# Two self-attention blocks of a perceiver kernel put into one hand-written schedule, batch by batch

## The chip, the cores and the metric

The kernel runs on one core of a Trainium2 chip. Its time is the device time in microseconds (us) of one execution; where several executions were timed, their median. One more execution was recorded by the hardware profiler: the profile has a record of every instruction on each engine. TensorE (PE in the profile) does the matrix products and transpositions, VectorE (DVE) and ScalarE (ACT) elementwise work and reductions, GpSimd (POOL) elementwise work on SBUF alone, SyncE (SP) asks for the transfers. Each engine works through its own list of instructions in the order of the program, and waits on semaphores for what others produce.

## What is computed

Six blocks in a row change an activation `x` of 4 batches x 256 tokens x 256 features, all in float32. The first four (a cross attention, a small self attention across batches, a mixture of experts, a second cross attention over 4096 keys) are not touched. The last two, cut to what matters:

```python
# fifth block, on z = _layernorm(x)
x_norm = layer_norm(z, g1, beta1)
q, k, v = heads(x_norm @ Wq + bq), heads(x_norm @ Wk + bk), heads(x_norm @ Wv + bv)   # 16 heads of 16
q, k = apply_rope(q), apply_rope(k)
attn = jax.nn.softmax(jnp.einsum('bhqd,bhkd->bhqk', q / jnp.sqrt(hd), k), axis=-1)
y = z + jnp.einsum('bhqk,bhkd->bhqd', attn, v) @ Wo + bo
x = x + y + jax.nn.relu(layer_norm(y, g2, beta2) @ W1 + b1) @ W2 + b2
# sixth block, on z = _layernorm(x): the same attention without the rotation, then a mixture of 8 experts
y = z + layernorm(attention(z) @ Wo + bo, g1, be1)
gate_probs = jax.nn.softmax(y @ Wg + bg, axis=-1)
top_vals, top_idx = jax.lax.top_k(gate_probs, 2)
x = x + y + layernorm(sum over the two of top_vals * (y @ We[e] + bexp[e]), g2, be2)
```

## The kernel before

Tokens lie in 8 tiles of 128, two to a batch. The blocks run one after the other (`build`, L1280), and the fifth and sixth are `l1_attn` (L1115) and `l1_ffn` (L1190). Each works stage by stage over all 8 tiles: norm, transposition, projections, attention, output projection, norm, and then the feed-forward network or the experts. Outside the attention the order of the instructions is left to a scheduler; inside `manual_schedule` it is the order in which the program writes them.

A norm (`normed`, L183) takes statistics of each tile on DVE (L190, L191), an inverse root for all tiles at once (`rsqrt`, L167: an addition, a Sqrt on ACT at L174, a reciprocal and one step of correction, L175 to L180), and applies both (L194). The Sqrt needs other activation tables than the exponential, so the program has ACT_TABLE_LOAD instructions on ACT. `transposed` (L202) turns tiles on TensorE.

`self_attention` (L306) goes through 16 units, one for each batch and each group of four heads. A step of its loop has two halves (`quad`, L316): in each, TensorE computes the scores of two heads of unit i (L327) and, for two heads of unit i + 2, the products from which DVE takes negated maxima (L333, L340). The exponentials follow on ACT (L338). Between the halves TensorE turns the maxima of unit i + 1 and the shares of an older unit (`turned`, L287), DVE adds the maxima to the queries (qm, L373), and the sums of unit i - 2 are formed (`sums`, L290, with a copy on POOL at L301). After the second half the probabilities of unit i - 1 weigh the values (`weigh`, L345). In PSUM three banks rotate for the scores, three (`mm_tile`) for everything that is called mm, which the maxima share with all projections, and one each for `acc` and `nm`. The output projection (`project_out`, L386) of two tiles at a time is the only other work inside the loop.

In `l1_attn` the rotation (`rotated`, L1128) multiplies with two weights each, adds biases and turns on DVE (L1146), and adds on POOL (L1156, L1157). The matrix products of all projections are recorded at one line, L165 in `contract`. In `l1_ffn` the affine part of a norm runs on POOL and DVE (L1217 to L1219), the gates are a softmax and a choice of two (`top2`, L222), and the experts' results are added on DVE (L1267). The output is written in one transfer at the end (L1289).

## Time and profile before

| | us |
|---|---|
| median of 3 runs | 2502.66 |
| lowest and highest | 2499.27, 2503.89 |
| the profiled execution: its time | 2499.59 |
| the profiled execution: its span | 2497.8 |
| last matrix product of the block before the two | 1996.8 |
| attention of the fifth block | about 2065 to 2158 |
| attention of the sixth block | about 2271 to 2357 |

A float32 product is recorded as two instructions, so counts of matrix products are twice those of the program. In a row of the timeline stand the start, the duration, the engine, line and operation, what is written and read, and in brackets how long the engine had been idle before it and who ended that. In the table by windows each engine's busy time stands with its number of instructions, then the share of its full clock that TensorE was granted (PEclk), the mean busy share of the transfer engines, and GB/s.

### The profile page before, as it was taken

Reading aid. Unit: us, or ns where it says so; the run is one execution under the profiler, and the core shown is the slowest. Engines: PE = TensorE matmul, PEld = TensorE weight load, DVE = VectorE, ACT = ScalarE, POOL = GpSimd, SP = SyncE. Lnnn points to the kernel's source line nnn. Section 1 sums busy time; section 2 is a strip of 40 time slices with the busy share of each in tenths; the row PEclk is TensorE's granted clock in tenths of the full one; section 3 lists DMA queues with packets and bytes.
Section 4 is the critical chain, followed back from the end, with each engine's and each line's share of the span. In section 5 each row is a group of like instructions: output and inputs, shape, how many; then the busy total and the mean of one; then the engine's idle time right before and its main releaser. Section 6 shows DMA issues by size and latency. Waiting matters only on the chain.

```text
span 2497.8 us, 45306 instructions
## 1 busy us (share of the span) xinstructions
PE 2276.8 (91%) x19032; PEld 1357.6 (54%) x19032; DVE 1204.5 (48%) x2197; ACT 948.1 (38%) x1838; POOL 147.6 (6%) x263
## 2 busy tenths in 40 slices
PE   7999983799997699999999999999999979899976
PEld 5777751487774245445544555455544536565642
DVE  2221248601222286666666666666666156525555
ACT  1100010122332326665566656665555604314400
POOL 0000000120001000000000000000000032100022
PEclk9888985599998899999999999999999987999968
DMA  4112011710112411221022101211100020010000
GB/s 133 56 51 68 17 64 49 272 66 15 34 32 63 131 53 40 66 62 36 27 62 62 45 27 45 70 54 36 32 23 2 2 76 10 1 43 1 2 1 17
DMA packets 82272, 121.36 MB, mean 49 GB/s; under 512 B 5371, under 2 KB 52243, under 8 KB 82068
## 3 DMA queue, kind: packets, MB, share of 16 engines
q1 hardware_dynamic: 80532, 114.25, 14.7%
q0 software_dynamic: 1536, 4.20, 0.5%
q8 instruction: 151, 2.47, 0.4%
q14 instruction: 53, 0.43, 0.1%
HBM read 109.19 MB, written 9.24 MB: 47 GB/s over the span
## 4 chain that ended last, share of the span: by engine, by line
PE 85%; DVE 6%; issue 3%; POOL 2%; ACT 2%; DMA 1%; SPq 0%; DVEq 0%; POOLq 0%; ACTq 0%
PE sc L1001 13%; PE acc L1052 10%; PE mx L1014 8%; PE h L165 8%; PE v L909 5%; PE k L909 5%; PE gram L425 5%; PE ro L165 4%; PE we L165 2%; PE eo L165 2%; PE po L165 2%; PE kv L165 2%; PE sc L327 2%; PE xo L165 1%; PE q L165 1%
## 5 line engine op out<-in xcount | busy, mean ns | idle before, releaser
L1043 DVE TENSOR_REDUCE mx<-mx 128x1 f32<-128x512 f32 x988 | 636.5, 686 | 408.8 <-PE mx L1014 368.2
L1039 ACT ACTIVATE probs<-sc 128x512 f32<-128x512 f32 x988 | 536.8, 597 | 420.5 <-PE mx L1014 394.3
L1001 PE MATMUL sc<-qm,kT 32*128 32x256 f32 x3952 | 579.1, 400 | 8.8 <-ACT probs L1039 8.8
L1014 PE MATMUL mx<-kT,x_q 32*128 32x512 f32 x1976 | 559.2, 639 | 0.0
L1001 PEld LDWEIGHTS sc<-qm,kT 32*128 32x128 f32 x3952 | 351.3, 184 | 254.9 <-ACT probs L1039 129.0
L1052 PE MATMUL acc<-probs,v 128*32 128x256 f32 x4096 | 274.9, 385 | 0.0
L1052 PEld LDWEIGHTS acc<-probs,v 128*32 128x32 f32 x4096 | 107.2, 109 | 134.3 <-issue 89.4
L1014 PEld LDWEIGHTS mx<-kT,x_q 32*128 32x128 f32 x1976 | 149.8, 183 | 8.1 <-issue 7.6
L909 PE MATMUL k<-slab,x_wk 128*32 128x512 f32 x1024 | 137.7, 623 | 12.3 <-DMA slab<-in_ctxT 7.4
L909 PE MATMUL v<-x_wv,slab 128*32 128x256 f32 x2048 | 137.0, 385 | 0.0
L425 PE MATMUL gram<-ctx 128*128 128x257 f32 x512 | 113.8, 381 | 3.6 <-POOL kv L454 2.4
L210 PE MATMUL tr<-ident,xn 128*128 128x128 f32 x112 | 30.0, 432 | 93.7 <-DVE xn L585 40.7
L425 PEld LDWEIGHTS gram<-ctx 128*128 128x128 f32 x512 | 96.1, 190 | 18.9 <-issue 2.9
L340 DVE TENSOR_REDUCE negm<-mx 128x2 f32<-128x512 f32 x128 | 82.9, 686 | 38.8 <-PE mx L333 38.1
L255 ACT ACTIVATE kT<-k,cols 128x512 f32<-128x512 f32 x128 | 92.8, 783 | 22.5 <-PE k L909 22.5
L301 POOL COPY wide<-rec 128x256 f32<-128x256 f32 x48 | 19.1, 399 | 1354.2 <-DVE rec L299 1354.2
L338 ACT ACTIVATE probs<-sc 128x512 f32<-128x512 f32 x128 | 69.7, 595 | 67.5 <-PE mx L333 56.5
L909 PEld LDWEIGHTS v<-x_wv,slab 128*32 128x32 f32 x2048 | 53.4, 109 | 73.0 <-issue 44.2
L165 PE MATMUL h<-f_w_all,rT 128*128 x184 | 83.0, 594 | 0.7 <-DVE rT L799 0.6
L165 PE MATMUL ro<-f_w_all,hT 128*128 x368 | 83.3, 379 | 0.1
L823 ACT ACTIVATE hT<-hT,place 128x128 f32<-128x128 f32 x184 | 49.9, 383 | 77.8 <-PE hT L820 77.7
L210 PEld LDWEIGHTS tr<-ident,xn 128*128 128x128 f32 x112 | 20.7, 211 | 102.6 <-issue 46.4
(325 smaller groups left out, 2718.2 us busy)
## 6 DMA issues: line engine op xcount, KB each, us to landing
slab<-in_ctxT SPq DMA_DIRECT2D x96, 512.0 KB
ctx<-in_ctx SPq DMA_DIRECT2D x16, 1024.0 KB
f_w_all<-in_f_W_r SPq DMA_DIRECT2D x16, 1024.0 KB
w<-in_f_W_s SPq DMA_DIRECT2D x4, 1024.0 KB
f_rows<-f_zero SPq DMA_DIRECT2D x1, 2944.0 KB
row<-f_rows SPq DMA_DIRECT2D x23, 128.0 KB
f_results<-y SPq DMA_DIRECT2D x23, 128.0 KB
kT<-x_away SPq DMA_DIRECT2D x128, 8.0 KB
```

The source lines that it names most:

```text
L165: nc.tensor.matmul(out, w, m, start=i == 0, stop=i == len(pairs) - 1)
L210: nc.tensor.transpose(ps[:, k * P : (k + 1) * P], src[:, 4 * q + k, c * P : (c + 1) * P], self.ident)
L255: nc.scalar.activation(dst, ps, AF.Identity, bias=b, scale=own)
L338: nc.scalar.activation(probs[i, j], sc[j][:, 0, :], AF.Exp, scale=0.25)
L340: nc.vector.tensor_reduce(negm[i2 % 2][:, :, 32 * j + UNIT_MAX[i2 % 2]], bd[j].rearrange("p (t s) -> p t s", s=S), AX.X, ALU.max, negate=True,
L425: nc.tensor.matmul(prod[:, m, : D + 1], t[:, c, m * P : (m + 1) * P], t[:, c, :], start=n == 0 and c == 0, stop=n == 3 and c == 7,)
L909: nc.tensor.matmul(out[own], w[:, own], m, start=start, stop=not start, tile_position=(0, 32 * j))
L1001: nc.tensor.matmul(into[:, c * S : (c + 1) * S], kT[b, u, at // HALF][rows, at % HALF : at % HALF + P], qm[un][rows, :], start=True, stop= ...
L1014: nc.tensor.matmul(into, q[rows, b, u, t * P : (t + 1) * P], kT[b, u, at // HALF][rows, at % HALF : at % HALF + SLAB], start=True, stop=True,)
L1039: nc.scalar.activation(probs[j], sc[j], AF.Exp, scale=0.25)
L1043: nc.vector.tensor_reduce(mx[un2][:, k2 % 2, j, k2 // 2 : k2 // 2 + 1], bd[j], AX.X, ALU.max)
L1052: nc.tensor.matmul(acc[32 * j : 32 * j + 32, :S], v[b, chunk // VC][:, at : at + 32], probs[j][:, c * S : (c + 1) * S], start=k == 0 and c ...
```

## The change

`self_attention`, `l1_attn` and `l1_ffn` go, with `project_heads` and `values_of_tokens`, and `l1_self` takes their place. It is one `manual_schedule` for both blocks. All weights of both are asked for at its start. The attention loop is the same as before in its matrix products, but it has 32 units in a row: the 16 of the fifth block, then the 16 of the sixth. All other work of a batch is written as three generators: `before_first` (norms, transposition, rotated queries and keys, values), `after_first` (output projection, norm, feed-forward, norm of the sixth block, its projections) and `after_second` (output projection, norm, gates, experts, last norm, output of two tiles). Each `yield` ends a piece, and gives its planned TensorE time and the planned delay until the next piece of the same generator may follow.

A small planner chooses while the program is written. `now` is a clock of planned times: a half step counts 1.07, the turning and sums 1.0, weighing 1.0. Between the two halves of a step, `between(7.0)` takes pieces that are due, from the first three generators, until 7 us are planned or none is due. `through` takes pieces until a given generator is done, before the first step that needs it. Steps are counted from -2 to 35 (two before the first unit, four after the last).

Norms are taken for the two tiles of a batch. Their inverse root is exp(-0.5 ln(v)) on ACT with the same step of correction on DVE (`inverse_root`). The second norm of the fifth block's input takes its variance from the first one's instead of statistics of its own. Transpositions are evacuated by ACT alone. Of the experts' results the odd ones are scaled by ACT and added by POOL; the affine part of the last norms works on both tiles at once. The output leaves in four transfers.

```diff
-    def self_attention(self, pool, q, k, v, out, project):
...
-    def values_of_tokens(self, pool, w, xT):
...
-    def l1_attn(self, x):
...
-    def l1_ffn(self, x):
...
+    def l1_self(self, x, out):
...
+            names = ("a1_wq", "a1_wqs", "a1_wk", "a1_wks", "a1_wv")
+            wq1, wqs1, wk1, wks1, wv1 = (self.load_w(pool, n) for n in names)
             turns = self.load(pool, "turns", [P, 2, 2, S], a["turns"].rearrange("p (h t s) -> p h t s", h=2, t=2))
...
+            def inverse_root(var, eps=EPS):
+                shape = [P, var.shape[1]]
+                new = lambda i: pool.tile(shape, F32, tag=f"ir{i}", name=self.name(f"ir{i}"), bufs=3)
+                ve, s, r, t = (new(i) for i in range(4))
+                nc.vector.tensor_scalar(ve, var, eps, None, ALU.add)
+                nc.scalar.activation(s, ve, AF.Ln)
+                nc.scalar.activation(r, s, AF.Exp, scale=-0.5)
+                nc.vector.tensor_mul(t, r, r)
+                nc.vector.tensor_mul(t, t, ve)
+                nc.vector.tensor_scalar(t, t, -0.5, 1.5, ALU.mult, ALU.add)
+                nc.vector.tensor_mul(r, r, t)
+                return r
+            def moments(src):
+                stats = pool.tile([P, NB, 6], F32, tag="st", name=self.name("st"), bufs=3)
+                mv = pool.tile([P, NB, 2], F32, tag="mo", name=self.name("mo"), bufs=3)
+                for t in range(NB):
+                    nc.vector.bn_stats(stats[:, t, :], src[:, t, :])
+                    nc.vector.bn_aggr(mv[:, t, :], stats[:, t, :])
+                return mv, inverse_root(mv[:, :, 1])
+            def apply(src, mv, r, dst):
+                for t in range(NB):
+                    nc.vector.tensor_scalar(
+                        dst[:, t, :], src[:, t, :], mv[:, t, 0:1], r[:, t : t + 1], ALU.subtract, ALU.mult
+                    )
...
+            def rotated(dst, ws, biases, xT, m, one):
+                ps = self.mm_tile("ro")
+                for i, w in enumerate(ws):
+                    heads(w, xT, m, ps[:, i * S : (i + 1) * S])
+                for half in range(2):
+                    u = 2 * m + half
+                    ts = []
+                    for i, bias in enumerate(biases):
+                        t = tile(f"ro{i}", [P, S], 2)
+                        nc.vector.scalar_tensor_tensor(
+                            t, ps[:, i * S : (i + 1) * S], self.col(bias, u), turns[:, half, i], op0=ALU.add, op1=ALU.mult
+                        )
+                        ts.append(t)
+                    if one:
+                        nc.gpsimd.tensor_scalar(ts[1], ts[1], self.col("one", half), None, ALU.add)
+                    nc.gpsimd.tensor_add(dst[:, u, :], *ts)
...
+            def before_first(b):
+                z = zs[0, b] = tile("z", [P, NB, D], 5)
+                mv, r = moments(own(b))
+                apply(own(b), mv, r, z)
+                vz = pool.tile([P, NB], F32, tag="vz", name=self.name("vz"), bufs=3)
+                nc.vector.tensor_mul(vz, r, r)
+                nc.vector.tensor_mul(vz, vz, mv[:, :, 1])
+                r2 = inverse_root(vz)
+                zn = tile("n", [P, NB, D], 4)
+                for t in range(NB):
+                    nc.scalar.activation(zn[:, t, :], z[:, t, :], AF.Copy, scale=r2[:, t : t + 1])
+                yield 0.0, 9.0
+                zT = turn(zn, "a1_g1", "a1_be1")
+                yield 0.5, 1.5
+                q[0, b], k[0, b] = (tile(n, [P, UNITS, S], 3) for n in "qk")
+                for m in range(DC):
+                    rotated(q[0, b], (wq1, wqs1), ("a1_bq", "a1_bqs"), zT, m, False)
+                    yield 1.8, 0.0
+                    rotated(k[0, b], (wk1, wks1), ("a1_bk", "a1_bks"), zT, m, True)
+                    yield 1.8, 0.0
+                values((0, b), wv1, zT)
+                yield 1.8, 4.0
+            def after_first(b):
+                ps = projected((0, b), wo1, ob1)
+                y = tile("y", [P, NB, D], 2)
+                nc.vector.tensor_add(flat(y), ps, flat(zs.pop((0, b))))
+                nc.gpsimd.tensor_add(flat(own(b)), flat(y), flat(own(b)))
+                mv, r = moments(y)
+                yn = tile("n", [P, NB, D], 4)
+                apply(y, mv, r, yn)
+                yield 4.4, 7.0
...
+                nc.vector.tensor_add(flat(own(b)), ps, flat(own(b)))
+                z = zs[1, b] = tile("z", [P, NB, D], 5)
+                mv, r = moments(own(b))
+                apply(own(b), mv, r, z)
+                yield 3.9, 6.0
...
+            def after_second(b):
+                ps = projected((1, b), wo2, ob2)
+                o = tile("n", [P, NB, D], 4)
+                nc.scalar.copy(flat(o), ps)
+                both = lambda n: affine[:, n, :].unsqueeze(1).to_broadcast([P, NB, D])
+                def affine_norm(src, n, residual, dst):
+                    mv, r = moments(src)
+                    nc.gpsimd.tensor_tensor(residual, residual, both(n + 1), ALU.add)
+                    apply(src, mv, r, src)
+                    nc.vector.tensor_tensor(src, src, both(n), ALU.mult)
+                    nc.gpsimd.tensor_tensor(dst, src, residual, ALU.add)
+                y = tile("y", [P, NB, D], 2)
+                affine_norm(o, 0, zs.pop((1, b)), y)
+                yield 4.4, 9.0
+                yT = turn(y)
+                nc.gpsimd.tensor_tensor(own(b), own(b), y, ALU.add)
...
+                nc.vector.tensor_add(flat(moe), flat(moe), flat(other))
+                affine_norm(moe, 2, own(b), own(b))
+                nc.sync.dma_start(out[:, NB * b : NB * (b + 1), :], own(b))
+                yield 0.0, 0.0
...
+            now, tasks = [0.0], []
+            def begin(work, key):
+                tasks.append([work, now[0], key])
+            def piece(task):
+                try:
+                    cost, lag = next(task[0])
+                    now[0] += cost
+                    task[1] = now[0] + lag
+                except StopIteration:
+                    tasks.remove(task)
+                    return False
+                return True
+            def between(time):
+                end = now[0] + time
+                while now[0] < end:
+                    ready = [t for t in tasks[:3] if t[1] <= now[0]]
+                    if not ready:
+                        break
+                    piece(ready[0])
+            def through(key):
+                while any(t[2] == key for t in tasks):
+                    at = next(i for i, t in enumerate(tasks) if t[2] == key)
+                    ready = [t for t in tasks[: at + 1] if t[1] <= now[0]]
+                    if ready:
+                        piece(ready[0])
+                    else:
+                        now[0] = min(t[1] for t in tasks[: at + 1])
+            UN = 2 * B * UNITS
+            where = lambda i: ((i // (B * UNITS), i // UNITS % B), i % UNITS)
...
+            with self.tc.manual_schedule():
+                for b in range(B):
+                    begin(before_first(b), ("first", b))
+                through(("first", 0))
+                for i in range(-2, UN + 4):
+                    if i + 2 < UN:
+                        (side, b), u = where(i + 2)
+                        if u == 0:
+                            through(("first", b) if side == 0 else ("mid", b))
+                    quad(i, True)
+                    ps = self.ps_o.tile([P, 512], F32, tag="f", name=self.name("nm"))
+                    if 0 <= i + 1 < UN:
+                        maxima = self.turned(ps, negm[(i + 1) % 2])
+                    if 0 <= i - 3 < UN:
+                        shares = self.turned(ps[:, S:], recs.pop(i - 3))
+                    if 0 <= i + 1 < UN:
+                        key, u = where(i + 1)
+                        qm[i + 1] = tile("qm", [P, S], 2)
+                        nc.vector.tensor_add(qm[i + 1], maxima, q[key][:, u, :])
+                    if 0 <= i - 3 < UN:
+                        key, u = where(i - 3)
+                        if u == 0:
+                            att[key] = tile("att", [P, UNITS, S], 2)
+                        nc.vector.tensor_mul(att[key][:, u, :], os.pop(i - 3), shares)
+                    if 0 <= i - 2 < UN:
+                        recs[i - 2] = self.sums(pool, accs.pop(i - 2), os[i - 2])
+                    now[0] += 1.0
+                    if 0 <= i - 3 < UN:
+                        (side, b), u = where(i - 3)
+                        if u == UNITS - 1:
+                            begin(after_first(b) if side == 0 else after_second(b), ("mid" if side == 0 else "last", b))
+                            tasks[-1][1] += 1.0
+                    between(7.0)
+                    quad(i, False)
+                    if 0 <= i - 1 < UN:
+                        weigh(i - 1)
+                while tasks:
+                    through(tasks[0][2])
...
-BLOCKS = ["l0_xattn", "l0_attn", "l0_ffn", "l1_xattn", "l1_attn", "l1_ffn"]
...
+BLOCKS = ["l0_xattn", "l0_attn", "l0_ffn", "l1_xattn"]
...
-        nc.sync.dma_start(tiled(out), x)
+        net.l1_self(x, tiled(out))
```

In the pieces left out, the feed-forward network is four pieces of 1.8 and two of 3.9 (the second of these with the norm shown), plain queries, keys and values 1.8 each, the gates 1.3 with a delay of 6.0, their transposition 0.5, the biases 1.0, and the experts eight pieces of 1.8.

## The prediction

> **What bounds the kernel now.** I read the page first, for which engine is full and where it is not, then a table of the tail by stage (the change touches nothing before it), then the order of time in the gaps.
>
> ```profile
> PE 2276.8 (91%) x19032; PEld 1357.6 (54%) x19032; DVE 1204.5 (48%) x2197; ACT 948.1 (38%) x1838; POOL 147.6 (6%) x263
> PE   7999983799997699999999999999999979899976
> PEclk9888985599998899999999999999999987999968
> ```
>
> TensorE is the bound; the last eight slices show where it is not full. The cross attention's last projection ends at 1996.9 us, so the two blocks own 2497.8 - 1997 = 501 us. By stage (busy us of each engine, granted clock):
>
> ```profile
> core 0: us, PE busy (x) PEld busy (x) DVE busy (x) ACT busy (x) POOL busy (x), PEclk, DMA share, GB/s
> 2008.00:2043.00 35.00, 32.49 (x95) 18.18 (x96) 20.49 (x35) 1.85 (x5) 9.95 (x8) 0.90 0.12 39
> 2043.00:2065.00 22.00, 11.19 (x24) 4.09 (x24) 8.35 (x13) 0.00 (x0) 16.89 (x12) 0.85 0.12 36
> 2065.00:2158.00 93.00, 91.31 (x924) 62.00 (x925) 59.19 (x126) 41.49 (x80) 15.16 (x24) 0.89 0.01 1
> 2174.00:2239.00 65.00, 65.00 (x224) 41.22 (x223) 11.97 (x31) 10.99 (x16) 0.00 (x0) 0.97 0.00 0
> 2357.00:2388.00 31.00, 16.31 (x91) 9.65 (x89) 17.78 (x36) 5.09 (x11) 15.18 (x21) 0.75 0.00 1
> 2388.00:2407.00 19.00, 12.99 (x54) 12.27 (x54) 6.21 (x15) 2.12 (x3) 3.86 (x6) 0.50 0.00 0
> 2476.00:2497.80 21.80, 0.00 (x0) 0.00 (x0) 14.54 (x26) 0.21 (x1) 12.77 (x16) 0.55 0.15 48
> ```
>
> Attention (fourth line) and feed-forward (fifth) fill TensorE already. What a merge can win is the rest: the rotation that waits for POOL (third), the norms between stages, gates at half clock (seventh), and a last norm with TensorE empty (eighth). The timeline prices one norm and one table load:
>
> ```profile
> 2370.16 0.37 ACT L1211 COPY o<-po 128x256 f32<-128x256 f32 x1 [2.18 <-PE po L165]
> 2370.55 1.28 ACT L174 ACT_TABLE_LOAD   x1
> 2371.84 0.21 ACT L174 ACTIVATE rs<-rs 128x8 f32<-128x8 f32 x1
> ...
> 2477.64 0.17 DVE L173 TENSOR_SCALAR rs<-mv 128x8 f32<-128x8 f32 x1
> 2477.84 0.21 ACT L174 ACTIVATE rs<-rs 128x8 f32<-128x8 f32 x1 [7.32 <-DVE rs L173]
> ...
> 2479.13 5.11 DVE L194 TENSOR_SCALAR o<-o,mv,rs_out 128x256 f32<-128x256 f32 x8
> ```
>
> An inverse root is seven small instructions in a row, 2479.13 - 2477.64 = 1.49 us. A load takes 1.28 us, and the next activation follows at once.
>
> **TensorE's work, which stays.** Attention: a step repeats every 4.37 us (the additions into qm start at 2092.95, 2097.32, 2101.69), so 32 x 4.37 = 140. All other work keeps its columns, at the full-clock prices of the chain's rows: experts 8 tiles x 7.06 = 56.5; output projections 16 x 2.24 = 36; feed-forward 61.6; rotated q and k 16 x 1.72 = 27.5; plain q and k 14; values 2 x 7.2 = 14.4; gates 5.7 (half of the 11.5 at half clock); biases 3.5; 64 transpositions at 0.15 = 9.4. Sum 228.6, together 368. Nothing uncovered would end at 1997 + 368 = 2365.
>
> **What is removed**: the waits between stages, 501 - 368 = 133 us of today's tail. The question is how much comes back. Before there were 6 inverse roots, each for 8 token tiles; now there are 24, each for 2 tiles: two in each of the four first norms, four more per batch. They are in the hand order, so TensorE waits in line behind them.
>
> **The inverse root by Ln and Exp** is again seven instructions (five DVE, two ACT), 1.49. What it does to the tables no row shows. From below: no load, if Ln and Exp share a set. From above: a load before each Ln and each Exp, 48 x 1.28 = 61.6 us of ACT. The Ln's load is done early, since ACT reaches it with nothing else to do (as at 2370.55, during the copy's follow-up on DVE); the Exp's stands between Ln and Exp, on the chain: 1.49 + 1.28 = 2.77. [...] The trace only shows loads placed per function at hand (L174, L1239, L174 each have their own), and the edit asks for no particular set, so I take 2.77, and keep 1.49 as a rival. [...]
>
> **Norm chains** for 2 tiles: statistics 0.43 + 0.18 + 0.31 + 0.08 = 1.0; root 2.77; application 0.42 + 0.33 = 0.75: 4.5 us. A first norm: 1.0 + 2.77 + 0.75 + 0.35 + 2.77 = 7.65, plus 0.8 for its ACT scaling.
>
> **Start.** (a) First norm before TensorE has anything: 0.4 + 7.65 + 0.8 = 8.9. Today it is 11.5 (1996.8 to 2008.3). (b) Half clock after that wait, as at 2006 to 2018: 3.5.
>
> (c) **The three other first norms.** All four generators begin at time 0 and their first piece costs the planner nothing, so in step -2 all three run between the low and the high half. DVE then does 3 chains in a row before the high half's maxima: 7.65 + 2 x 8.55 (the ACT scaling and next Ln load delay the later ones by 0.9) = 24.8, and 0.7 for the first maximum. TensorE has one half step of matmuls and then no free bank: 25 lost. (d) It restarts at half clock, with matmuls of 32 rows that do not lift it (0.50 from 2062 to 2084 today): two steps took 11.6 there for 8.7, and the next pieces start slow as well: 9.
>
> (e) **Norms inside the row.** Following the planner's costs through the loop, a norm piece is the last filler of its step in nearly every case (steps 7, 11, 12, 15, 16, 19, 20, 23, 24, 26, 30, 31). Behind it on DVE stand the high half's maxima (0.69 each), behind it on ACT its exponentials; TensorE waits for both, since three mm banks rotate and the next low half needs the first high one back. For the eight in the first block's second part: addition 0.7, chain 4.5, maximum 0.7 = 5.9, minus the high half 1.07, the weighing 1.0 and the first matmuls 0.4: 3.4 lost, 27. The four of the second block add an affine product and have less cover: 4.3 each, 17. (That product, 512 wide and new, lies between 0.69, any 512-wide row of DVE, and 1.9, twice L1218 beside a busy POOL; POOL has nothing to do then, so 0.7.) Sum 44. [...]
>
> (f) **Clock after such stalls.** Today's rotation shows two idle stretches like these: 3.76 us before 2050.12 (clock stays 1.00) and 3.66 before 2057.45 (0.55 next). [...] The rows have one of two falling: 10.
>
> (g) **End.** Only the last batch's second part is left, and it is serial: waiting for the gates of the third batch behind two norm chains 9, for its last norm before the fourth batch's transposition is evacuated 4, top 2 of the fourth with hand-overs 5, final norm with POOL's addition 8, last 256 KB written 4 (1 MB takes 5.4 today; three quarters are written under other work), half clock after two of these 6: 36. Today's end is 22, its gate stage 19.
>
> (h) **Queues.** SP: all weights are asked for at the start; the second output row needs 5.0 MB, at 360 GB/s (2002 to 2010) 14 us after 1998 against 8 for the first matmuls; 3 if it stands ahead, taken between 0 and 6. POOL: four rotation pieces need 4 x 0.8 + 8 x 0.65 = 8.4 us (half of the 512-wide rows L1156, L1157) beside 7.2 on TensorE: 1 per batch, 4. Evacuations moved to ACT, the ReLUs and the expert scaling are free: ACT has 32 x 2.76 for attention, 62 of loads and some 70 for the rest, 220 of 500 us. Sum 7.
>
> **Sum.** 8.9 + 3.5 + 25 + 9 + 44 + 10 + 36 + 7 = 143. End 1997 + 368 + 143 = 2508; with 1.8 outside the span (2499.59 - 2497.8) 2510. The profiled run lies 3.1 under the median of 2502.66, so **2513**: the old 133 us of waiting go, and 143 new ones come.
>
> **Rivals.**
> 1. [...] 0.2.
> 2. The pieces cover the norms as the planner's due times intend: (e) 10, (f) 2. Then 2513 - 42 = 2471, faster. For it: 228 us of filler exist. Against: a norm piece is last in its step, and DVE works in order. 0.18.
> 3. The clock stays low. TensorE's half steps use 32 rows, which held 0.50 for 20 us at 2062. If each of 12 stalls costs 4 us, (f) is 48: 2551. It decides from a granted clock under 0.85 between 2080 and 2400. For it: that window. Against: filler of 128 rows follows, which brought 1.00 back within 4 us at 2176. 0.2.
>
> The likeliest sum has 0.42, own range 2502 to 2525. A measurement of this kernel can tell about 0.2% (5 us) from no change. Faster by more: rivals 1 and 2, 0.38. Within: the lower edge of the likeliest, 0.1. Slower: the rest of it and rival 3, 0.52. Range 2464 to 2550: from both rivals' times less the 7 of (h), up to rival 3.
>
> **What would show it.** Step (c): TensorE idle some 25 us around 2020 to 2047. Table loads: 48 more ACT rows of 1.28, or one. Step (e): matmuls mx waiting 3 to 5 us for the negm reductions in twelve steps. Step (g): TensorE's last matmul about 12 us before the end. I am wrong if the first attention step comes before 2035, if there are few loads, or if mx waits under 2 us after norms.

## The result and the profile after

The changed kernel takes 2613.2 us (median of 4 runs, 2611.9 to 2616.2), the kernel before on the same chip 2501.0: ratio 1.0451, 95% interval 1.0432 to 1.0469. It is slower by 112 us. The forecast of 2513 had the sign and not the size, and its range ended at 2550. The sign is little merit: the prediction gave slower only 0.52. The kernel before was timed again beside each group of experiments, with medians of 2501.5 to 2503.4, so it moved little from group to group.

The page of the changed kernel, the same three rows as before:

```profile
PE 2334.2 (89%) x19192; PEld 1414.1 (54%) x19192; DVE 1191.2 (46%) x2283; ACT 1041.4 (40%) x1996; POOL 163.6 (6%) x297
PE   8999874799995899999999999999997698888976
PEclk9888885799997999999999999999998688888877
```

In the last ten slices (from 1958 us) TensorE's digits are 6 to 9 and its clock's 8 and less. So two things were lost, time and clock. The table by windows divides the new schedule in three: the start (from the last score product of the cross attention to the first addition into qm), the row of attention steps (to the last such addition), and the end.

```profile
core 0: us, PE busy (x) PEld busy (x) DVE busy (x) ACT busy (x) POOL busy (x), PEclk, DMA share, GB/s
1989.60:2064.30 74.70, 34.24 (x152) 18.96 (x150) 26.61 (x98) 32.17 (x50) 10.94 (x17) 0.69 0.32 106
2064.30:2476.20 411.90, 361.54 (x2379) 248.62 (x2380) 172.86 (x416) 146.63 (x278) 59.18 (x93) 0.86 0.00 1
2476.20:2610.40 134.20, 89.74 (x297) 48.84 (x296) 51.22 (x152) 39.69 (x72) 33.42 (x37) 0.75 0.03 8
```

To weigh the two against each other I cut the tail (all that follows the cross attention) into slices of 1 us and split each into TensorE's idle time, the **clock loss** (busy time x (1 - granted clock)) and the rest, which is work at full clock. The three add up to the time.

| from the end of the cross attention | idle | clock loss | work at full clock | all |
|---|---|---|---|---|
| before, from 1997 | 80.7 | 36.9 | 383.4 | 501 |
| forecast | 114.5 | 28.5 | 368 | 511 |
| after, from 2000 | 133.6 | 77.8 | 398.7 | 610 |

(In the forecast's row the clock is (b), (d), (f) and 6 of (g).) The change made TensorE idle for 53 us more, and 41 us more went to a lower clock. That is 94 of the 109 us; the other 15 are called work, although the products are the same. Most of them go when the waits go (386.0 in the experiment e10_defer), so they are perhaps waits that the record counts as busy; no run shows it.

Who waits for what in this tail (TensorE; sum, times, longest):

```profile
PE mx L1335 <- DVE negm L1343: 32.8, 11, 24.0
PE sc L1329 <- ACT probs L1341: 19.9, 12, 2.2
PE h L165 <- ACT h L1176: 9.0, 16, 0.6
PE ph L165 <- DVE q L254: 5.1, 4, 1.3
PE ph L165 <- DVE k L254: 5.1, 4, 1.3
PE ob L165 <- DMA f_wo<-in_f_wo: 3.5, 1, 3.5
```

The one wait of 24.0 is step (c), the three first norms in step -2. The other ten for negm and the twelve for probs come to 28.7 us: 25.9 of them stand behind the ten norms in the row, 2.2 behind an eleventh just after it, and one wait of 0.6 has no norm ahead of it. The next three lines, 19.2 us, no part of the forecast had: the ReLU pieces and the q and k pieces write both halves of one PSUM tile, and TensorE's second half starts only when the first has been evicted (the waits of h for ACT, 0.56 us each, and of ph for DVE, 1.23 to 1.29). The timeline shows one norm of the row (step 15):

```profile
2260.15 0.20 ACT L1054 ACTIVATE ir<-ir 128x2 f32<-128x2 f32 x1 [9.10 <-DVE ir L1053]
2260.37 1.28 ACT L1055 ACT_TABLE_LOAD   x1
2261.67 0.20 ACT L1055 ACTIVATE ir<-ir 128x2 f32<-128x2 f32 x1
2261.78 1.06 ACT L1341 ACTIVATE probs<-sc 128x512 f32<-128x512 f32 x2
2262.41 0.48 PE L1329 MATMUL sc<-qm,k 32*128 32x256 f32 x1 [1.94 <-ACT probs L1341]
2264.09 0.79 PE L1335 MATMUL mx<-k,q 32*128 32x256 f32 x1 [0.98 <-DVE negm L1343]
```

ACT sits in line behind the norm: Ln, load, Exp, and only then the exponentials for which TensorE waits, first 1.94 and then 0.98 us. The same stretch by windows of 3.4 us:

```profile
2257.40:2260.80 3.40, 3.07 (x36) 1.00 0.00 0
2260.80:2264.20 3.40, 0.81 (x8) 0.88 0.00 0
2264.20:2267.60 3.40, 3.40 (x18) 0.50 0.02 5
2267.60:2271.00 3.40, 3.40 (x11) 0.62 0.00 0
```

(Columns: window, length, TensorE busy, granted clock, the transfers' share and GB/s.) The stall of 2.9 us is followed by 6.8 us at half clock. This happens after every one of the ten norms between 2064 and 2476, for 6.8 or 10.2 us each. Of the clock loss in the row about 38 us lie behind these norms (2150 to 2476), 7 in the restart after step -2 (2064 to 2080), and 7 behind short waits for the rotation of the next batches (2090 to 2131), of 1 to 1.8 us, for which no part of the forecast had a price.

### The profile page after: what moved, and what is told of

It is laid out like the page before. It is cut to its first block, busy times and chain, and to the rows that moved or that the text cites. A ratio compares the mean times of both kernels' runs of the same rounds, so it can differ in the third digit from the quotient of the medians.

```text
span 2610.4 us, 45762 instructions
## 1 busy us (share of the span) xinstructions
PE 2334.2 (89%) x19192; PEld 1414.1 (54%) x19192; DVE 1191.2 (46%) x2283; ACT 1041.4 (40%) x1996; POOL 163.6 (6%) x297
## 4 chain that ended last, share of the span: by engine, by line
PE 83%; DVE 8%; ACT 4%; issue 3%; DMA 1%; POOL 1%; SPq 1%; POOLq 0%; ACTq 0%; DVEq 0%
PE sc L913 13%; PE acc L964 9%; PE h L165 8%; PE mx L926 8%; PE v L821 5%; PE k L821 4%; PE gram L337 4%; PE ro L165 4%; PE we L165 2%; PE po L165 2%; PE eo L165 2%; PE kv L165 2%; PE sc L1329 2%; PE mx L1335 1%; PE xo L165 1%
## 5 line engine op out<-in xcount | busy, mean ns | idle before, releaser
L955 DVE TENSOR_REDUCE mx<-mx 128x1 f32<-128x512 f32 x988 | 636.6, 686 | 412.6 <-PE mx L926 369.7
L1335 PE MATMUL mx<-k,q 32*128 32x256 f32 x512 | 105.2, 469 | 38.5 <-DVE negm L1343 32.8
L337 PE MATMUL gram<-ctx 128*128 128x257 f32 x512 | 113.8, 381 | 3.6 <-POOL kv L366 2.4
L1329 PE MATMUL sc<-qm,k 32*128 32x256 f32 x512 | 96.3, 453 | 19.9 <-ACT probs L1341 19.9
L337 PEld LDWEIGHTS gram<-ctx 128*128 128x128 f32 x512 | 96.1, 190 | 18.9 <-issue 2.9
L1335 PEld LDWEIGHTS mx<-k,q 32*128 32x128 f32 x512 | 62.7, 215 | 50.9 <-DVE negm L1343 39.6
```

The costliest lines, as they stand in the source:

```text
L337: nc.tensor.matmul(prod[:, m, : D + 1], t[:, c, m * P : (m + 1) * P], t[:, c, :], start=n == 0 and c == 0, stop=n == 3 and c == 7,)
L955: nc.vector.tensor_reduce(mx[un2][:, k2 % 2, j, k2 // 2 : k2 // 2 + 1], bd[j], AX.X, ALU.max)
L1329: nc.tensor.matmul(sc[j][:, c * S : (c + 1) * S], k[key][rows(j), u, c * P : (c + 1) * P], qm[i][rows(j), :], start=True, stop=True,)
L1335: nc.tensor.matmul(bd[j][:, c * S : (c + 1) * S], q[key][rows(j), u, c * P : (c + 1) * P], k[key][rows(j), u, :], start=True, stop=True,)
```

## The experiments

In all runs "changed" is the changed kernel. Stages are those above; idle and clock loss are TensorE's in the row of attention steps.

| run | median us | against changed | start | row | idle in row | clock loss in row | end |
|---|---|---|---|---|---|---|---|
| changed | 2613.2 | | 74.7 | 411.9 | 50.4 | 51.5 | 134.2 |
| e1_one_set | 2572.4 | -40.8 | 65.4 | 392.7 | 38.0 | 44.4 | 125.9 |
| e2_own_banks | 2584.6 | -28.6 | 77.4 | 384.4 | 31.8 | 48.1 | 134.5 |
| e3_early_norms | 2597.3 | -15.9 | 63.8 | 412.6 | 50.1 | 51.9 | 133.9 |
| e4_norm_first | 2622.7 | +9.5 | 81.9 | 406.5 | 54.9 | 55.0 | 143.6 |
| e5_rows_later | 2605.6 | -7.6 | 64.0 | 418.7 | 49.9 | 54.6 | 134.0 |
| e6_sqrt | 2581.6 | -31.6 | 66.6 | 393.8 | 40.6 | 46.9 | 132.1 |
| e7_busy | 2574.0 | -39.2 | 76.3 | 377.4 | 30.3 | 14.0 | 134.2 |
| e8_all | 2539.5 | -73.7 | 52.7 | 369.8 | 18.7 | 42.6 | 127.5 |
| e9_all_busy | 2506.7 | -106.5 | 55.4 | 340.8 | 7.6 | 11.0 | 121.9 |
| e10_defer | 2499.4 | -113.8 | 52.5 | 335.2 | 13.6 | 21.8 | 122.9 |
| e11_tail | 2539.7 | -73.5 | 55.4 | 367.5 | 19.0 | 39.2 | 127.4 |
| e12_best | 2497.5 | -115.7 | 52.7 | 331.9 | 13.6 | 18.4 | 122.9 |

How far one profile's stage can be trusted: the start is the same program in changed, e2, e4 and e7, and took 74.7, 77.4, 81.9 and 76.3, because the block before ended at different times. The first addition into qm itself came at 2064.3 to 2066.4 in these four. So the start is better judged by it: 2050.6 in e1, 2047.7 in e3, 2051.0 in e5, 2056.5 in e6 and 2040.0 in e8.

**e1_one_set.** One load of a set with both functions, placed ahead of the first norm:

```diff
+            with self.tc.issue_after(self.last_copy.ins):
+                nc.scalar.preload_act_table_set("natural_log_exp_and_others")
             with self.tc.manual_schedule():
```

> The changed kernel with one more instruction: ACT loads, once, ahead of the last block's first norm, the table set that holds both Ln and Exp, so that the 48 loads in its profile become 1; every norm's chain gets 1.28 us shorter and each of the twelve norms in the row of attention steps releases the exponentials queued behind it earlier. Theory A (the loss against the kernel before is made of four things of like size: stalls behind norms with the half clock that follows each, waits between two halves of one PSUM bank, the weights that the second output row waits for, and the end): 25 to 40 us less than the changed kernel's 2613, so 2573 to 2588, still 3% slower than before; the TensorE stall after a norm goes from about 2.9 to about 1.6 us, and some of the twelve half-clock stretches vanish. Rival B (the table loads are the cause, everything else is hidden): under 2510. Rival C (loads are beside the point: it is the wait for DVE's maxima that drops the clock): under 10 us less.

Measured 2572.4, ratio to before 1.0287 (1.027 to 1.0305). The two waits of the row and of step -2:

```profile
PE mx L1335 <- DVE negm L1343: 23.7, 11, 14.4
PE sc L1329 <- ACT probs L1341: 5.4, 8, 1.0
```

The wait for the exponentials falls from 19.9 to 5.4 us and step -2's from 24.0 to 14.4. The loads cost 41 us, at the upper end of theory A. B falls, since without them the kernel is still 2.9% slower than before, and so does C. The clock loss in the row moves little (51.5 to 44.4): behind shorter stalls (for the exponentials 1.0 us at the longest, 2.2 in the changed kernel) the clock still falls.

**e2_own_banks.**

```diff
-                    ps = self.mm_tile("h1")
                     for i in range(2):
-                        part = ps[:, i * S : (i + 1) * S]
+                        part = self.mm_tile("h1")[:, :S]
```

and the same for q and k. 

> The changed kernel, with each half of the ReLU pieces (h1) and of the q and k pieces in a PSUM tile of its own instead of two halves in one tile; the same matmuls and evictions. Theory A (TensorE's second half waits until the first half's eviction is read from the same bank: 0.56 us in each of 16 h1 pieces, 1.29 us in each of 8 q and k pieces of the row, and the clock falls after the longer of them): 18 to 30 us less than the changed kernel's 2613, so 2583 to 2595; the waits of h for ACT and of ph for DVE vanish, a step with four h1 pieces takes 11.6 instead of 14.4 us, a step with q and k about 12 instead of 17. Rival B (the evictions set the pace, the waits only move to the next piece that asks for a buffer): under 5 us less, with the same time waiting for a free tile.

Measured 2584.6, ratio 1.0332 (1.0313 to 1.035). The three lines of h and ph are gone from the waits and nothing stands in their place: the idle time in the row falls by 18.6 us, which is their 19.2. The row becomes 27.5 shorter; the rest is 3.4 us of clock loss and less time called work. Theory A holds.

**e3_early_norms.**

```diff
                 for b in range(B):
                     begin(before_first(b), ("first", b))
+                for task in tasks[:3]:
+                    piece(task)
+                tasks[1][1] = tasks[2][1] = 35.0
                 through(("first", 0))
```

> The changed kernel, with the first norms of batches 1 and 2 asked for directly after batch 0's first norm, ahead of batch 0's own projections, and batch 3's left where it was. Theory A (three norms in one step hold up DVE and ACT for 24 us with TensorE idle; two of them can lie in the time in which the first norm and the output rows leave TensorE idle anyway): the idle stretch of 24 us goes to 6 to 10 us and some of it comes back as a later first transposition; 8 to 18 us less than 2613, so 2595 to 2605. Rival B (the start is bound by the weights for the second output row, so that DVE and ACT have time there): the whole 24 us less two thirds, 16 us less and nothing given back, 2597. Rival C (the norms just move the stall ahead): no change, 2610 to 2616.

Measured 2597.3, ratio 1.0383 (1.0365 to 1.04). The whole gain lies at the start: the first addition comes 16.6 us earlier, row and end stay. The longest wait for negm falls from 24.0 to 6.7, and 2.7 us come back in the first rotation, which waits longer for ACT's evacuation (3.4 instead of 0.7). Theories A and B both allow this size; what is given back speaks for A, and C falls.

**e4_norm_first.** Each norm was cut from the piece that feeds it and made the first piece of the next filler:

```diff
                 nc.gpsimd.tensor_add(flat(own(b)), flat(y), flat(own(b)))
+                yield 4.4, 0.5
                 mv, r = moments(y)
                 yn = tile("n", [P, NB, D], 4)
                 apply(y, mv, r, yn)
-                yield 4.4, 7.0
+                yield 0.0, 6.0
```

and the same for the two other norms. 

> The changed kernel, with each norm of the row of attention steps split off from the projection or sum that feeds it, and made the first piece of the next step's filler, so that filler of 7 us stands on TensorE between the norm and the next exponentials and maxima. Theory A (what is lost in the row comes from norms whose chain on DVE and ACT stands directly ahead of an attention half step, with no filler behind them to keep TensorE busy, and from the half clock that follows): 25 to 60 us less than 2613, so 2553 to 2588; most of the twelve half-clock stretches after norms vanish. Rival B (pieces behind the norm need DVE or ACT themselves, h1's ReLUs above all, so the stall just moves into the filler): within 10 us of 2613.

Measured 2622.7, ratio 1.0486 (1.0468 to 1.0503): 9.5 us slower than changed, so theory A as I put it falls. The wait for the exponentials goes down (19.9 to 11.4, the third line here), but the first two are new:

```profile
PE tr L1082 <- POOL y L1216: 11.2, 1, 11.2
PE tr L1082 <- DVE z L1072: 9.7, 2, 4.9
PE sc L1332 <- ACT probs L1344: 11.4, 7, 2.0
```

The norm came later and the transposition that needs it stayed close behind it in the hand order, 20.9 us. The stall did move into the filler as B said, but through the transposition and not the ReLUs. By stages the row is 5.4 us shorter and the end, where the wait of 11.2 stands, 9.4 longer; the first addition comes as in changed. As tried here, a norm first in the next filler shifts the stall more than it removes it; e10 tries another order.

**e5_rows_later.**

```diff
-            ob1, b2 = self.output_row(wo1, "a1_bv", "a1_ob"), self.row("a1_b2")
+            row1, b2 = self.row("a1_ob"), self.row("a1_b2")
...
+                if b == 0:
+                    output_row(wo1, "a1_bv", row1)
                 ps = projected((0, b), wo1, row1)
```

and the same for the second row. 

> The changed kernel, with the two output rows (nine matmuls each on weights that land 9 and 18 us after the block before ends) computed by the pieces that first need them instead of ahead of the first transposition. Theory A (between the end of the block before and the first transposition TensorE waits for these weights and not for the norm, which is done after 8 us): the first transposition comes about 10 instead of 21.9 us after the last projection of the block before, the rows' own 8 us of matmuls return later as filler, and 9 to 13 us are gained: 2600 to 2604. Rival B (the first norm and the half clock are what costs, the weights are hidden behind them): under 4 us. Rival C (the three norms of the step before the row just wait longer): no gain, 2610 to 2616.

Measured 2605.6, ratio 1.0413 (1.0396 to 1.0431): 7.6 us, between A and B. The first transposition comes at 2006.3 instead of 2021.6, as A said, and the first addition 13.3 us earlier; the row becomes 6.8 longer, since the rows' own matmuls come back there. The wait for the weights is worth 7 us, not the 15.6 by which the first transposition in changed came later than the 1997 + 8.9 of the forecast.

**e6_sqrt.** The form of the norm alone undone:

```diff
-                nc.scalar.activation(s, ve, AF.Ln)
-                nc.scalar.activation(r, s, AF.Exp, scale=-0.5)
+                nc.scalar.activation(s, ve, AF.Sqrt)
+                nc.vector.reciprocal(r, s)
```

> The changed kernel with the norm form of the kernel before: square root on ACT and reciprocal on DVE in place of Ln and Exp; all else stays. So it undoes one part of the change. Theory A (as built, Ln and Exp come from two table sets, so that a norm still loads two tables; the form brought nothing): the number of loads falls from 48 to about 30, since norms that follow one another keep the square root's table; the chain of a norm loses a load but the next exponentials get one ahead of them; 5 to 20 us less than 2613, so 2593 to 2608, most of it ahead of the row. Rival B (the Ln and Exp form does save something against the square root): over 2618.

Measured 2581.6, ratio 1.0312 (1.0294 to 1.0331). ACT's loads in the tail of this run:

```profile
L1054 ACT ACT_TABLE_LOAD x16 | 20.5, 1283 | 0.3
L1341 ACT ACT_TABLE_LOAD x13 | 16.7, 1283 | 0.2
L1232 ACT ACT_TABLE_LOAD x2 | 2.6, 1283 | 0.0
```

31 loads instead of 48, as expected, but 31.6 us instead of my 5 to 20. None stands within a norm's chain any more; the ten waits for negm in the row (8.8 us) are gone, while those for the exponentials stay (18.9), because now the exponentials have the load ahead of them. So Ln and Exp as built cost more than the square root, and B is refuted.

**e7_busy.** Extra products whose results are not used, behind those that a norm follows:

```diff
+            def warm():
+                ps = self.ps_o.tile([P, 512], F32, tag="f", name=self.name("warm"))
+                for i in range(6):
+                    nc.tensor.matmul(ps[:, :D], wo1[:, 0, :P], w1[:, 0, :D], start=True, stop=True)
```

> The changed kernel, with six more matmuls of 128x256 (0.43 us each at full clock, results not read) behind the matmuls of each projection and sum that a norm follows, so that TensorE works instead of standing still while DVE and ACT do the norm. It computes nothing that is used. Theory A (a large part of the loss in the row of attention steps is the half clock that follows each stall of 2 to 3.5 us, and not the stalls themselves): time at half clock in the row goes from 113 us to under 60, and although 12 x 2.6 us of matmuls are added the kernel gets 15 to 35 us faster: 2578 to 2598. Rival B (the clock falls for other reasons, the two halves of a bank or the load itself): half clock stays above 90 us and the time is 2610 to 2640. Rival C (the stalls are longer than this work, so they remain as stalls of half the length, and the clock falls all the same): 2605 to 2615.

Measured 2574.0, ratio 1.028 (1.0259 to 1.0301): 39 us **faster** with 72 more matmuls, some 29 us of work, and more than theory A's 15 to 35. The row of this run:

```profile
2066.40:2443.80 377.40, 347.14 (x2499) 242.74 (x2499) 170.30 (x415) 148.09 (x278) 59.15 (x93) 0.96 0.00 1
```

The granted clock is 0.96 instead of 0.86. In the row 23.1 us of work came in, 20.1 us of idle time and 37.5 us of clock loss went out, so that it is 34.5 shorter. The work that came in is more than the idle time that it filled; the gain is the clock alone. Behind the norms 3 us of clock loss are left of 38. So the clock behind the stalls, and not only the stalls, is what the new order costs. Rivals B and C fall.

**e8_all.** e1, e2, e3 and e5 together. 

> The changed kernel with four edits together: one table set, own banks for the halves of h1, q and k, early norms of batches 1 and 2, and the output rows later. Theory A (four separate losses): the sum of what they gave alone is 41 + 29 + 16 and about 11 us expected of the rows; the three that act ahead of the row overlap by 10 to 15 us, so 75 to 95 us less than 2613: 2518 to 2538, still slower than the kernel before by 0.6 to 1.4%. Rival B (the losses hang together through the clock, which stays up once the stalls are short enough): under 2505, no slower than before. Rival C (what one edit frees another wait takes): over 2550.

Measured 2539.5, ratio 1.0147 (1.013 to 1.0165): 73.7 us, just short of theory A's 75 to 95. Singly the four gave 92.9, so 19 us are missing. All of it is missing at the start: there the first addition came 43.6 us earlier in the single runs taken together, and 24.3 here, where the first rotation now waits 9.6 us for ACT. The row gave 39.2 singly and 42.1 together, the end 8.5 and 6.7. B falls here: with only 18.7 us of idle time left in the row, the clock loss is still 42.6, 29 of it behind norms.

**e9_all_busy.** e8 with e7's extra products, four at each norm:

```diff
-                for i in range(6):
+                for i in range(4):
```

> The four edits together (e8_all, 2539.5 us) and, behind the matmuls of each projection and sum that a norm follows, four more matmuls of 128x256 whose results are not used. Theory A (what is left of the loss in the row of attention steps is mostly half clock after short stalls: 86 us at half clock with only 18.7 us of TensorE idle): half clock in the row falls under 40 us and 15 to 28 us are gained, although 16 x 1.7 us of matmuls are added: 2512 to 2525. Rival B (stalls of 1 to 1.6 us do not bring the clock down, its falls have another cause): half clock stays over 70 us and the time is over 2540.

Measured 2506.7, ratio 1.0021 (1.0013 to 1.0029): 32.8 us from e8, more than the 15 to 28 expected; there are 12 such places and not 16, so less work was added. The clock loss in the row falls from 42.6 to 11.0, and behind the norms none is left. So the short stalls at the norms of e8 (single waits of 0.5 to 1.7 us) are what brought it down there; what remains is the restart and the rotation.

**e10_defer.** e8 with each norm of the row queued behind the half step that follows, without added work:

```diff
-                mv, r = moments(y)
-                yn = tile("n", [P, NB, D], 4)
-                apply(y, mv, r, yn)
+                yn = tile("n", [P, NB, D], 4)
+                def norm():
+                    mv, r = moments(y)
+                    apply(y, mv, r, yn)
+                later.append(norm)
                 yield 4.4, 7.0
...
                     if 0 <= i - 1 < UN:
                         weigh(i - 1)
+                    flush()
```

> The four edits together (e8_all, 2539.5 us) and each norm of the row put off: its projection or sum stays where it is, but the norm's work on DVE and ACT is queued behind the exponentials, the maxima and the weighing of the half step that follows, with no added work. Theory A (the order is what makes a norm cost anything: queued ahead of the exponentials it stalls TensorE, behind them its 3 us lie beside the weighing and the next half step's matmuls, 2.1 us, and the next filler): TensorE's idle time in the row falls by 5 to 12 us and with it half clock; 10 to 28 us gained: 2512 to 2530. Rival B (it stalls the next half step instead): within 5 us of 2539.

Measured 2499.4, ratio to before 0.9986 (0.9978 to 0.9994): 40 us from e8, more than theory A's 10 to 28. The waits in its row that are left, but for some short ones (the second line, the rotation's, is the same in all these runs):

```profile
PE ph L165 <- DVE negm L1365: 5.4, 4, 2.0
PE mx L1357 <- DVE ro L1122: 4.2, 3, 1.8
PE mx L1357 <- DVE negm L1365: 2.7, 2, 1.7
PE sc L1351 <- ACT probs L1363: 0.6, 1, 0.6
```

In e8 the exponentials and maxima held TensorE 4.5 and 9.3 us there. Only 5.1 us of idle time are saved, but 20.8 us of clock loss; behind the norms it goes from 29 us to 8. The products are the same, so here the order of the instructions on ACT and DVE makes the difference. Against the kernel before, this tail has less idle time (70 us for 80.7), more clock loss (44 for 36.9) and as much work: the merge as repaired exchanges one for the other.

**e11_tail and e12_best.** The last pieces of two batches in turn:

```diff
-                while tasks:
-                    through(tasks[0][2])
+                while tasks:
+                    ready = [t for t in tasks[:2] if t[1] <= now[0]]
...
```

> The four edits together (e8_all, 2539.5 us), and after the last attention step the last pieces of two batches at a time are taken in turn, as they come ready, where before each batch was worked off by itself, its waits for its norm and its gates with nothing beside them. Theory A (the end is made of waits of one batch's chain, 38 us of idle TensorE and the half clock after them, which another batch's experts can fill): the end from the last attention step falls from 127.5 to 90 to 105 us: 2502 to 2517. Rival B (DVE, ACT or POOL set the pace of the experts): under 8 us gained.

> The four edits, the norms put off, and two batches taken in turn at the end. Theory A (what the last two gain lies in different stages and adds up): 35 to 60 us less than 2539.5, so 2480 to 2505, no slower than the kernel before (2501) and probably faster by up to 0.8%. Rival B (they share a bound): over 2515.

Measured 2539.7 and 2497.5 (ratio 0.9986, 0.9977 to 0.9995). The edit, which also gave the transposed gates a second buffer, did nothing: the order on every engine came out as it was, apparently because by the planner's own times the first batch always had a piece due. So e11 is a second run of e8 and e12 one of e10, and they agree within 0.2 and 2 us. The idea itself stays untried. e10 and e12 lie 0.14% below the kernel before. Their intervals just leave out 1, but the difference is less than the 0.2% that the prediction set as its bound, so I call them no faster.

## Why the prediction was wrong, step by step

**Right.** 48 loads, one on each chain (the root from the variance to the result took 2001.73 to 2004.44, 2.71 against 2.77). Step (c): 24.0 us idle against 25. Rival 1 did not come: a load stands between each of the 24 pairs of Ln and Exp, and e1, where they are gone, is 40.8 us faster. The rotation of (h): 5.7 us of waits against 4, though not the clock behind them. The restart (d): 9 us, of which the row shows 7. Step (e) had the right mechanism, its price was above the mark: 25.9 us of stalls behind the ten norms of the row, 2.6 each, where I had 44 for twelve. Of its two waits the larger is for the exponentials on ACT, not for the maxima; I had written that a wait of mx under 2 us would prove me wrong, and it is under 2 us after norms, but ACT holds TensorE up in its place.

**(f), the clock, is the step that failed.** I took 10 us for twelve stalls and named two idle stretches of the old rotation, of which one was followed by half clock (columns as in the first table by windows):

```profile
2046.00:2050.00 4.00, 0.36 (x1) 0.00 (x0) 1.53 (x3) 0.00 (x0) 3.10 (x3) 1.00 0.00 0
2050.00:2054.00 4.00, 3.67 (x8) 1.44 (x8) 1.61 (x3) 0.00 (x0) 3.19 (x3) 1.00 0.01 2
2054.00:2058.00 4.00, 0.55 (x2) 0.34 (x3) 1.87 (x4) 0.00 (x0) 2.44 (x2) 1.00 0.22 66
2058.00:2062.00 4.00, 3.40 (x6) 0.94 (x4) 1.38 (x2) 0.00 (x0) 3.85 (x3) 0.55 0.10 19
```

In the row of attention steps all ten norms were, and the low clock lasted 6.8 or 10.2 us each time: about 38 us behind ten norms, 3.8 each. That these stalls cause it is shown by e7 and e9, where filling them leaves 3 and 0 us. No run shows the 10 us of (f): the two stretches show that the clock falls after one of them and not what a fall costs, which was my estimate; the runs show 3.8 us for each stall in its place. Rival 3 had 48 for twelve stalls, 4 each, and was the right size. I gave it 0.2 and weighed it by filler that brings the clock back within 4 us; behind the norms it took 6.8 or 10.2. Its test was badly set too: the granted clock from 2080 to 2400 is 0.88, over the 0.85 that I asked for, and the loss is there all the same.

**A term was missing: two halves in one tile.** The change takes the ReLU pieces and the q and k pieces of the row two at a time into one PSUM tile. I priced them by TensorE's columns only and called the ReLUs on ACT free. They cost 28.6 us (e2), 19.2 of it as idle time.

**(g), the end**, was 36 and is 63.3 (44.1 idle and 19.2 clock loss after the last addition into qm). I had only the last batch's second part left there; in the trace three of four batches' experts run after the row. The planner takes filler for 7 us in a step, and what does not fit or is not due is left for the end, after the attention steps.

**(h), the weights**, were 3 and are about 7 (e5). Of the 15.6 us by which the first transposition was late, 8 are the rows' own products.

**The work that stays** was 368 and measures 386 to 399. The same slices give 383.4 for the kernel before, so 15 us were missing from my count of the old trace: not 133 but 118 us of its tail are idle time and clock loss.

The sum: idle time and clock loss are 211 us instead of 143. The start has 46 against 41 (mostly (h)), the row 102 against 66, the end 63 against 36. In the row the clock took 33 more, the halves of a tile 19, other short waits 2, and the stalls at norms 18 less. With 31 more of work, and a tail that starts 3 later, this makes the 102 us between the forecast end of 2508 and 2610.

## What to carry to other kernels

Where two engines work in order behind one another, look not only at how long a chain is but at what is queued behind it: in the changed kernel a norm ahead of the exponentials cost TensorE a stall of 1.9 to 3.1 us and then half its clock for 7 to 10 us. Put behind them, with the other repairs in, the norms of the row went with 8 us of clock loss instead of 29. When work is merged so that TensorE is nearly full, price every short stall with the clock that follows it, from a stretch of the trace with the same kind of matmuls (here 3.8 us behind each). And try a PSUM tile of its own for each product that is evicted by itself; here that gave 28.6 us.

## What the runs showed of the hardware

The clock can fall after very little idle time. In e8_all TensorE waits 0.49 us in the middle of a half step of 32-row products, and is idle for 0.6 us in the two slices together (window, length, busy, granted clock):

```profile
2188.00:2189.00 1.00, 0.90 (x6) 1.00 0.00 0
2189.00:2190.00 1.00, 0.51 (x8) 1.00 0.00 0
2190.00:2191.00 1.00, 1.00 (x11) 1.00 0.00 0
2191.00:2192.00 1.00, 1.00 (x7) 0.57 0.00 0
```

Shortly after 2191 the clock is at half. The same wait at 2294.6 is followed by half clock too (0.50 from 2297), the one at 2242.8 is not (1.00 throughout). Idle time by itself does not decide it. In e10_defer the clock falls after 6.8 us without idle time in the record, filled by half steps of 32 rows, weighing, transpositions and products that write 4 or 8 columns (first two lines); in e7_busy waits of 1.29 us between products of 128 rows and 256 columns leave it at 1.00 (last two):

```profile
2328.80:2332.20 3.40, 3.40 (x28) 1.00 0.00 0
2332.20:2335.60 3.40, 3.40 (x9) 0.51 0.00 0
2211.00:2214.40 3.40, 2.10 (x13) 1.00 0.00 0
2214.40:2217.80 3.40, 2.11 (x11) 1.00 0.00 0
```

So idle time as the record counts it does not explain these falls alone, and the kind of product may matter too. Whether its rows, its columns or something else about it counts, no run separates. The stretches at half clock that begin in the row last 6.8 or 10.2 us in the changed kernel and 3.4 to 10.2 in e8_all; in the end of the changed kernel they last 10.2, 13.7 and 17.1.

A load of a table took 1.28 us, in both kernels, and where ACT had nothing else to wait for the next activation followed within 0.02 us (2260.37 above). In the kernel before the seven loads of the tail stand in turn at the square root (L174) and at an exponential (L338, L1239). In the changed kernel Ln and Exp got a load each, 24 at L1054 and 24 at L1055. In e1_one_set, which asks for one set by name, one load is left in the tail (at 1988.86), and the first Ln (1997.52) is followed by its Exp (1997.76) with none between them.

Where the changed kernel writes and evicts two halves of one PSUM tile in turn, the second half's product waits for the first half's eviction: 0.56 us behind ACT's ReLU, 1.23 to 1.29 us where ACT and then DVE evict. In e2_own_banks, with a tile for each half, these waits are gone. Whether the bank or the order kept for the tile does this, no run here tells.
